# Two attention blocks on one core: where the residual is added, and in which buffers it waits

## The chip, the core and the metric

The kernel runs on one core of a Trainium2 chip. Its engines work in parallel, each on its own queue of instructions: TensorE (PE; PEld is its loading of weights), VectorE (DVE), ScalarE (ACT), GpSimd (POOL) and SyncE (SP), which here issues every DMA. SBUF is the working memory, PSUM the memory that PE writes its products to. GpSimd does not touch PSUM in this kernel. The metric is the device time of one execution in microseconds; the median of several runs counts.

## The reference, cut to what matters

The input x has 8 images of 512 channels and 32 x 32 pixels. Two layers of the same kind follow one another; each is a group normalization, a projection to queries, keys and values, attention with 8 heads of 64 channels over the 1024 pixels, an output projection, and the addition of the layer's input, the residual:

```python
xn = group_norm(x)                       # 8 groups in layer 0, 32 in layer 1
q, k, v = split(qkv_w @ xn + qkv_b)      # each (512, 1024) per image
attn = softmax(q.T @ k / 8)              # per head, 1024 x 1024
out = proj_w @ (attn @ v) + proj_b
return out + x
```

All of it is in float32.

## The kernel before

**Units.** A unit is one layer of one image: units 0 to 7 are layer 0, units 8 to 15 are layer 1. Layer 0 writes its results to `mid` in DRAM, layer 1 to the output. The loop at L903 emits per unit: the values (`v`), the queries (`q`), the keys (`k`), then the output projection of the *previous* unit (`o`), and then the attention of this unit. The first unit has no `o`; the last unit's projection stands alone at the end.

**Products.** Each of v, q, k and o is a 512 x 512 by 512 x 1024 matrix product, done with seven block products in place of eight, in the order 1, 6, 2, 7, 5, 4, 3 (`ORDER`). In q, k and o each of the seven is again done with seven small matmul pairs (`Stream.product`, L411). A product uses one pair of PSUM banks for its main part (`main`, alternating between two pairs, a0 and a1) and another for a part that is the same for half of the result: that part is copied by ACT to the main banks as a seed (L426) and, for the seventh, to a small SBUF tile `late` (L438, three buffers). When the main part is complete, a `finish` step reads it from PSUM on VectorE, and GpSimd then adds `late` to half of the columns (`add_late`, L456 to L458). The tail of a product, with its finish, is emitted inside the product that follows, after that one's first matmul. I write o6 for product 6 of the projection and its finish.

**Sums.** The finishes at L460 to L496 build running sums: p1 (product 1 with bias), u2 = main 6 + p1, u3 = main 7 + bias + u2, and `wide` adds main 5 into u2. These three tiles share two buffers (`accpool`), which attention uses too.

**The output projection** (L537). Its result has four quarters (r, h): r is the half of the channels, h the half of the pixels. For each a tile res[r, h] (128 x 2 x 512) is first loaded with the residual (L546), then the terms are added into it, and it is stored (L558). `take` (L551) adds a product from PSUM on VectorE and `late` on GpSimd; `more` (L555) adds one of the sums, from SBUF to SBUF. Before, `more` runs on VectorE for quarter (0, 0) at o6 and for (0, 1) at o4, and on GpSimd for (1, 1) at o5 and (1, 0) at o4. Below, res10 is the tile of r = 1, h = 0, and so on.

**Buffers.** All four residual tiles come from `ppool`, which has five buffers, and from which come also the rooms xa and xb for combinations of the normalized input (last read by k3), one sum of the values, the rooms oa and ob for combinations of the attention output (last read by o7 and o3), and in attention the exponentials. `tmppool` (one buffer) holds xr, read last by k4, and in attention tmp, written first at step 8; `rbpool` (one buffer) holds the spread reciprocals rb, read last by the division at v5 and written next at step 21 of attention.

**Attention** (L685). 64 steps per unit: eight chunks (a pair of heads and half of the queries) of eight key blocks. A step has scores on PE (L711, eight matmuls), an exponential on ACT (L719) into a `ppool` tile of 128 x 1024, a product with the values on PE (L739, eight matmuls), and a sum of exponentials on VectorE (L758). At the start the order on PE is scores 0, 1, 2, product 0, scores 3, product 1, scores 4 and so on, with products 5 and 6 both ahead of scores 8. An empty PE instruction (`gate`, L108) carries waits that the order alone does not ensure. For step 0 it waits for everything that wrote q and k; in units after the first the keys are long complete then, in unit 0 they are the work just before.

**What sets the order.** It is written out by hand: functions are hung at products with `at(sel, k, ...)` and run after that product's finish, in the order of hanging. Every DMA goes through SP in program order, and an instruction that waits holds those behind it. Residual loads hang at k4, at k3 (two, behind two loads of the next input) and at o7. The statistics of the next input (`stats_of`, L256) hang at o1, o2, o7, o4 and o3. Units 1 to 4 also build a weight image for later units; its raw weights are loaded at L1063 (`load_raw`, four DMAs), between the last product and its tail.

Of the kernel before, what the change touches and what calls it, by code (L numbers as in the profile page):

```python
# [11 lines left out]
F32 = mybir.dt.float32  # L12
# [6 lines left out]
P = 128  # L19
# [13 lines left out]
def fast_path(ctx, tc, x, qkv_wT, proj_wT, vecs, groups, out, flag):  # L33
# [5 lines left out]
    nc = tc.nc  # L39
# [4 lines left out]
    FD = 512  # L44
# [19 lines left out]
    ppool = pool("ppool", 5)  # L64
    accpool = pool("accpool", 2)
    latepool = pool("latepool", 3)
    tmppool = pool("tmppool", 1)
    trpool = pool("trpool", 2)
    rbpool = pool("rbpool", 1)
# [49 lines left out]
    def on(engine, inst, tile_name, *banks):  # L119

        for other, its_engine, its_banks in seen[tile_name]:
            if its_engine != engine and not set(banks) & set(its_banks):
                tc.declare_no_dep(raw(inst), raw(other), reason="another bank of the pair")
        seen[tile_name].append((inst, engine, banks))
        return inst
# [29 lines left out]
    left_slots = [Left(t[:, :, :FD], t[:, :, FD:]) for t in slots]  # L155
# [5 lines left out]
    def load_raw(l, sel, left, ks=tuple(RAW), after=None):  # L161
        w = proj_wT[l] if sel == "o" else qkv_wT[l][:, "qkv".index(sel) * C : ("qkv".index(sel) + 1) * C]
        src = w.rearrange("(c p) o -> p c o", p=P)
        for k in ks:
            c, o = RAW[k]
            n = nc.sync.dma_start(left.outer(k), src[:, c : c + 2, o : o + FD2])
            if after is not None:
                follows(n, after, "x comes first")
                after = None
# [286 lines left out]
    def add_late(t, late):  # L456
        cols = in_two(t[:, 1, :])
        return nc.gpsimd.tensor_add(cols, cols, twice(late))  # L458
# [41 lines left out]
    def make_pairs(stream, w, sel, bias, left, early, hook):  # L500
        l, _ = units[w.u]
        tiles = getattr(w, sel + "p")
        st, p1, u2, u3, wide = sum_steps(l, bias, f"{sel}_{w.u}", early)
        w.last[sel] = []

        def result(r, h, more):
            def finish(main, m, late):
                to = tiles[r][:, :, ts(h, FD)]
                w.last[sel].append(on("DVE", nc.vector.tensor_add(to, main, st[more]), m, 0, 1))
                w.last[sel].append(add_late(to, late))  # L510

            return finish

        def fifth(main, m, late):
            to = tiles[1][:, :, FD:]
            for i in range(2):
                wide(main, m, i)
                w.last[sel].append(
                    on("DVE", nc.vector.tensor_add(to[:, i, :], main[:, i, :], st["u3"][:, i, :]), m, i)
                )  # L520
            w.last[sel].append(add_late(to, late))

        steps = {
            1: p1, 6: u2, 2: result(0, 0, "p1"), 7: u3, 5: fifth, 4: result(1, 0, "u3"),
            3: result(0, 1, "u2"),
        }
        for k in ORDER:
            if k == 1 and early is not None:
                continue

            def finish(main, m, late, k=k):
                steps[k](main, m, late)
                hook(sel, k)

            stream.product(left.quarters(k), w.right.inner[k], k == 3, finish)

    def project(stream, w, left, hook):  # L537
        l, b = units[w.u]
        src, dst = source_of(w.u), mid[b] if l == 0 else out[b]
        st, p1, u2, u3, wide = sum_steps(l, PB, f"o_{w.u}")  # L540
        add = nc.vector.tensor_add
        res = w.res = {}

        def load(r, h):
            t = res[r, h] = ppool.tile([P, 2, FD], F32, tag="p", name=f"res{r}{h}_{w.u}")
            nc.sync.dma_start(t, block_rows(src, r, h))  # L546

        w.load_res = load

        def take(r, h, main, m, late):  # L550
            on("DVE", add(res[r, h], main, res[r, h]), m, 0, 1)  # L551
            add_late(res[r, h], late)

        def more(r, h, name, engine=nc.vector):
            engine.tensor_add(res[r, h], res[r, h], st[name])  # L555

        def store(r, h):
            nc.sync.dma_start(block_rows(dst, r, h), res[r, h])  # L558

        def sixth(*args):  # L560
            u2(*args)
            more(0, 0, "p1")

        def second(*args):
            take(0, 0, *args)
            store(0, 0)

        def fifth(main, m, late):
            t = res[1, 1]
            for i in range(2):  # L570
                wide(main, m, i)
                on("DVE", add(t[:, i, :], main[:, i, :], t[:, i, :]), m, i)
            add_late(t, late)
            more(1, 1, "u3", nc.gpsimd)
            store(1, 1)

        def fourth(*args):
            take(1, 0, *args)
            more(1, 0, "u3", nc.gpsimd)
            store(1, 0)  # L580
            more(0, 1, "u2")

        def third(*args):
            take(0, 1, *args)
            store(0, 1)

        steps = {1: p1, 6: sixth, 2: second, 7: u3, 5: fifth, 4: fourth, 3: third}

        def product(k):
            def finish(main, m, late):  # L590
                steps[k](main, m, late)
                hook("o", k)

            stream.product(left.quarters(k), w.right_o.inner[k], k == 3, finish)

        return product
# [88 lines left out]
    def attention(w, at_step):  # L685
        u = w.u
# [5 lines left out]
        def scores(s):  # L692
            c, t = divmod(s, NT)
            pr, qh = divmod(c, NH)
            if s < 6:
                bank = (*sbank, apair[1])[s % 3]
                before = state["exp"][s - 3 : s - 2] if s >= 3 else []
            elif s == n_steps - 1:
                bank = apair[0]
                before = state["free"][0]  # L700
            else:
                bank = sbank[s % 2]
                before = [state["exp"][s - (3 if s < 8 else 2)]]
            if s < 3:
                before = before + [i for i, _, _ in seen[("s0", "s1", "a1")[s]]]
            if s == 0:
                before += w.last["q"] + w.last["k"]
            gate(*before)
            for j in range(2):
                for e in range(2):  # L710
                    nc.tensor.matmul(  # L711
                        bank[e * H : (e + 1) * H, j, :],
                        w.k[pr][j * H : (j + 1) * H, t * P + e * H : t * P + (e + 1) * H],
                        w.q[pr][j * H : (j + 1) * H, ts(qh, FD)],
                        start=True,
                        stop=True,
                    )
            p = ppool.tile([P, 2, FD], F32, tag="p", name=f"p_{u}_{s}")
            exp = nc.scalar.activation(p, bank, AF.Exp, scale=SCALE)  # L719
            state["exp"].append(exp)  # L720
            state["p"].append(p)
            return p
# [111 lines left out]
        for s in range(n_steps):  # L834
            c, t = divmod(s, NT)
            p = scores(s)
# [39 lines left out]
    first = {sel: mix_left(left) for sel, left in (("v", slot_v), ("q", slot_q), ("k", left_first_k))}  # L876
# [23 lines left out]
    MAKE = {1: (1, "v"), 2: (1, "q"), 3: (1, "k"), 4: (1, "o")}  # L900

    old = None
    for u in range(2 * B):  # L903
        w = Unit()
        w.u, w.right, w.last = u, right, {}
        l, _ = units[u]
# [3 lines left out]
        def at(sel, k, *parts):  # L910
            hooks.setdefault((sel, k), []).extend(parts)
# [124 lines left out]
        ahead = u if last else u + 1  # L1036
        at("k", 5, partial(load_xn, ahead, 0, 2))
        make_pairs(stream, w, "q", QB, lefts["q"], early["q"], hook)
        if u:
            product = project(stream, old, left_slots[1], hook)  # L1040
            at("k", 4, partial(old.load_res, 0, 0))
            at("k", 3, partial(load_xn, ahead, 2), partial(old.load_res, 1, 1), partial(old.load_res, 1, 0))
            at("o", 1, partial(stats_of, 0, 1))
            at("o", 2, partial(stats_of, 2))
            at("o", 7, partial(old.load_res, 0, 1), partial(stats_of, 3, 4))
            at("o", 4, partial(stats_of, 5))
            at("o", 3, partial(stats_of, 6, 7))
        else:
            at("k", 3, partial(load_xn, ahead, 2))
        make_pairs(stream, w, "k", KB, lefts["k"], early["k"], hook)  # L1050
        if u:
            for k in ORDER:
                product(k)
# [4 lines left out]

        right = Right(xn, xt) if not last else None
        making = [] if last else [None] * 8  # L1060
        make = MAKE.get(u)
        if make is not None:
            load_raw(*make, left_slots[0])  # L1063
            making = [part for parts_of in mix_left(left_slots[0])[: 1 if make[1] == "v" else 2] for part in parts_of]

        def at_step(s, state):
# [38 lines left out]
        old = w  # L1105
# [277 lines left out]
```

## Time and profile before

| | |
|---|---|
| median of three runs | 3258.51 us (3257.65 to 3258.57) |
| profiled execution, own time | 3261.41 us |
| its span, first to last instruction | 3259.6 us |
| PE busy | 3208.7 us (98%) |
| VectorE busy | 2862.9 us (88%) |
| ACT busy | 1890.5 us (58%) |
| GpSimd busy | 910.9 us (28%) |

The span is what the trace covers; an execution's own time has a little around it. Times inside the trace count from the span's start. In the rows of groups and of the timeline, `res<-res,u_o` means that a tile named res was written from res and from u_o; the last bracket is idle time of the engine before the instruction, with what ended it. The waits behind a semaphore are inferred from its updates. Busy time of PE is modelled for overlapping matmuls, so a stall can hide in it; the length of a stretch with a known number of steps is the surer measure.

### The profile page before, as it was taken

The numbers are of one execution on the slowest core, as the hardware profiler recorded it, in microseconds if no ns is written. First come the engines' busy times: TensorE is split into PE (matmuls) and PEld (weight loads), VectorE is DVE, ScalarE is ACT, GpSimd is POOL, SyncE is SP. The second block draws the span as 40 slices with busy tenths as digits, with TensorE's granted clock in tenths as the row PEclk, the third lists the DMA queues.
The fourth block names the chain that finished last, engine by engine and source line by source line (L and its number), as shares of the span: only waits on it lengthen the run. The fifth ranks groups of instructions, "written<-read, shape, count | busy, mean of one in ns | idle before, by whom it ended". The sixth has DMA issues, their size and how long they took to land.

```text
span 3259.6 us, 59781 instructions
## 1 busy us (share of the span) xinstructions
PE 3208.7 (98%) x22998; PEld 2087.4 (64%) x22998; DVE 2862.9 (88%) x3362; ACT 1890.5 (58%) x3077; POOL 910.9 (28%) x589
## 2 busy tenths in 40 slices
PE   9999999999999999999999999999999999999999
PEld 7366584765846658476584765857567585675843
DVE  7888989989889898988989889898898988889887
ACT  3655746557465574655656566574655746557454
POOL 5033051330513305133050431504214042240410
PEclk9999999999999999999999999999999999999999
DMA  5333242432424314233142331423323233232311
GB/s 194 107 110 125 78 144 89 145 126 97 141 84 146 123 56 145 77 109 114 52 151 77 106 125 45 156 68 113 115 75 127 74 116 105 85 124 76 127 57 48
DMA packets 151344, 344.83 MB, mean 106 GB/s; under 512 B 27152, under 2 KB 40976, under 8 KB 151056
## 3 DMA queue, kind: packets, MB, share of 16 engines
q1 hardware_dynamic: 151056, 340.94, 32.8%
q8 instruction: 186, 3.05, 0.4%
q14 instruction: 102, 0.84, 0.1%
HBM read 282.29 MB, written 57.02 MB: 104 GB/s over the span
## 4 chain that ended last, share of the span: by engine, by line
PE 89%; POOL 4%; DVE 3%; DMA 2%; ACT 1%; issue 1%; SPq 0%; ACTq 0%; DVEq 0%; POOLq 0%
PE a L739 25%; PE s L711 23%; PE s L421 17%; PE a L421 12%; PE a L398 6%; PE s L398 5%; POOL res L555 2%; POOL res L458 2%; DMA mid<-res 1%; DVE acc L758 1%; DMA out_dram<-res 1%; ACT p L719 1%; PE a L711 0%; PE s L664 0%; PE a L664 0%
## 5 line engine op out<-in xcount | busy, mean ns | idle before, releaser
L719 ACT ACTIVATE p<-s 128x1024 f32<-128x1024 f32 x976 | 997.2, 1024 | 560.6 <-PE s L711 457.0
L739 PE MATMUL a<-p,v 64*64 64x512 f32 x8192 | 1126.6, 590 | 33.8 <-ACT p L719 23.4
L711 PE MATMUL s<-q,k 64*64 64x512 f32 x7808 | 1084.1, 591 | 3.6 <-POOL k L458 3.6
L758 DVE TENSOR_TENSOR acc<-acc,p 128x1024 f32<-128x1024 f32 x768 | 951.6, 1239 | 90.5 <-ACT p L719 45.5
L739 PEld LDWEIGHTS a<-p,v 64*64 64x64 f32 x8192 | 407.5, 131 | 516.7 <-ACT p L719 389.5
L711 PEld LDWEIGHTS s<-q,k 64*64 64x64 f32 x7808 | 430.5, 133 | 390.6 <-issue 390.6
L426 ACT COPY a<-s 128x256 f32<-128x256 f32 x1308 | 465.5, 357 | 278.0 <-PE s L421 197.3
L939 POOL TENSOR_TENSOR k<-xn 128x512 f32<-128x512 f32 x16 | 20.3, 1270 | 1324.1 <-DVE xn L217 1324.1
L438 ACT COPY late<-s 128x256 f32<-128x256 f32 x327 | 121.8, 373 | 179.5 <-PE s L421 179.0
L398 PE MATMUL a<-w,xn 128*128 128x256 f32 x768 | 178.1, 381 | 0.0
L825 ACT ACTIVATE ao<-ao,vec 128x512 f32<-128x512 f32 x128 | 88.4, 715 | 146.9 <-DVE ao L818 146.9
L756 DVE TENSOR_TENSOR acc<-p,p 128x1024 f32<-128x1024 f32 x128 | 162.9, 1272 | 4.2 <-ACT p L719 4.2
L398 PEld LDWEIGHTS a<-w,xn 128*128 128x128 f32 x768 | 144.5, 190 | 31.4 <-issue 12.2
L770 DVE STREAM_TRANSPOSE tr<-acc 128x1024 f32<-128x1024 f32 x128 | 158.0, 1235 | 0.0
L778 DVE TENSOR_REDUCE red<-tr 128x32 f32<-128x1024 f32 x128 | 154.3, 1206 | 0.6
L421 PE MATMUL s<-xn,w 128*128 128x256 f32 x492 | 146.5, 379 | 0.0
L421 PE MATMUL a<-xn,w 128*128 128x256 f32 x492 | 146.4, 379 | 0.0
L421 PE MATMUL s<-k,w 128*128 128x256 f32 x492 | 146.3, 379 | 0.0
L421 PE MATMUL a<-xt,w 128*128 128x256 f32 x462 | 137.5, 379 | 0.0
L288 POOL TENSOR_TENSOR y<-var,half 128x4 f32<-128x4 f32 (+1 forms) x17 | 33.5, 1972 | 366.0 <-DVE var L286 366.0
L765 DVE TENSOR_TENSOR ao<-a,tmp 128x512 f32<-128x512 f32 x128 | 88.1, 688 | 48.9 <-ACT tmp L764 47.8
L421 PE MATMUL s<-xt,w 128*128 128x256 f32 x432 | 128.5, 379 | 0.0
(206 smaller groups left out, 4730.3 us busy)
## 6 DMA issues: line engine op xcount, KB each, us to landing
w<-iq SPq DMA_DIRECT2D x105, 448.0 KB, 3.4
w<-ik SPq DMA_DIRECT2D x105, 448.0 KB, 6.0
w<-io SPq DMA_DIRECT2D x105, 448.0 KB, 3.4
rb<-drec SPq DMA_DIRECT2D x128, 256.0 KB, 3.9
w<-iv SPq DMA_DIRECT2D x105, 256.0 KB, 2.9
xn<-mid SPq DMA_DIRECT2D x36, 512.0 KB, 3.8
xn<-x_dram SPq DMA_DIRECT2D x32, 512.0 KB, 4.2
res<-x_dram SPq DMA_DIRECT2D x32, 512.0 KB, 5.7
```

What stands on the lines that cost most here:

```text
L398: step()
L421: nc.tensor.matmul(dst, a[j], b[j], start=start, stop=j != 1, skip_group_check=True),
L426: n = nc.scalar.copy(dst, one)
L438: on("ACT", nc.scalar.copy(late, seventh), s, 1)
L711: nc.tensor.matmul(bank[e * H : (e + 1) * H, j, :], w.k[pr][j * H : (j + 1) * H, t * P + e * H : t * P + (e + 1) * H], w.q[pr][j * H : (j ...
L719: exp = nc.scalar.activation(p, bank, AF.Exp, scale=SCALE)
L739: nc.tensor.matmul(banks[r][j * H : (j + 1) * H, :], w.v[rows, t, lo : lo + D], p[rows, j, :], start=(t == 0), stop=(t == NT - 1),)
L756: nc.vector.tensor_add(acc, state["first"], p)
L758: nc.vector.tensor_add(acc, acc, p)
L770: nc.vector.transpose(tr, state["acc"].pop(c))
L778: nc.vector.tensor_reduce(red[:, :, qh, :], state["tr"].rearrange("p j (f i) -> p j f i", i=BL), AX.X, ALU.add)
L825: nc.scalar.activation(cols, cols, AF.Identity, bias=vec[:, units[u][0], VB, pr : pr + 1])
```

## The change

Four things change in the program.

1. The residual tiles: res10 now comes from `rbpool` and res01 from `tmppool`; res00 and res11 stay in `ppool`. All four are loaded by k3 (res00 at k4; at k3, behind the two input loads, res10, res11 and res01).
2. The sums: all four `more` additions run on GpSimd, and they come before the takes: p1 into res00 at o1, u2 into res01 at o6, u3 into res10 at o7; u3 into res11 stays at o5. Main 5, which went into u2 and from there into res01, is now added to res01 directly from PSUM at o5, so `wide` is not used there. The number of VectorE instructions at o5 is the same.
3. Two of the eight statistics hang one step earlier (2, 3 at o2; 4, 5 at o7; none at o4), and the raw weights of units 1 to 4 are loaded at o7.
4. The gate of step 0 leaves out the last two writes of the keys (the addition and the late addition of k3, which write pixels 512 to 1023); the gate of step 2 waits for them. Scores 0 to 3 read the first 512 pixels of the keys.

```diff
         def load(r, h):
-            t = res[r, h] = ppool.tile([P, 2, FD], F32, tag="p", name=f"res{r}{h}_{w.u}")
+            room, tag = {(1, 0): (rbpool, "rb"), (0, 1): (tmppool, "tmp")}.get((r, h), (ppool, "p"))
+            t = res[r, h] = room.tile([P, 2, FD], F32, tag=tag, name=f"res{r}{h}_{w.u}")
...
-        def more(r, h, name, engine=nc.vector):
-            engine.tensor_add(res[r, h], res[r, h], st[name])
+        def more(r, h, name):
+            nc.gpsimd.tensor_add(res[r, h], res[r, h], st[name])
...
+        def first(*args):
+            p1(*args)
+            more(0, 0, "p1")
+
         def sixth(*args):
             u2(*args)
-            more(0, 0, "p1")
+            more(0, 1, "u2")
...
+        def seventh(*args):
+            u3(*args)
+            more(1, 0, "u3")
+
         def fifth(main, m, late):
-            t = res[1, 1]
             for i in range(2):
-                wide(main, m, i)
-                on("DVE", add(t[:, i, :], main[:, i, :], t[:, i, :]), m, i)
-            add_late(t, late)
-            more(1, 1, "u3", nc.gpsimd)
+                for t in (res[0, 1], res[1, 1]):
+                    on("DVE", add(t[:, i, :], main[:, i, :], t[:, i, :]), m, i)
+            add_late(res[1, 1], late)
+            more(1, 1, "u3")
             store(1, 1)
 
         def fourth(*args):
             take(1, 0, *args)
-            more(1, 0, "u3", nc.gpsimd)
             store(1, 0)
-            more(0, 1, "u2")
...
-        steps = {1: p1, 6: sixth, 2: second, 7: u3, 5: fifth, 4: fourth, 3: third}
+        steps = {1: first, 6: sixth, 2: second, 7: seventh, 5: fifth, 4: fourth, 3: third}
...
             if s == 0:
-                before += w.last["q"] + w.last["k"]
+                before += w.last["q"] + w.last["k"][:-2]
+            elif s == 2:
+                before += w.last["k"][-2:]
...
-            at("k", 3, partial(load_xn, ahead, 2), partial(old.load_res, 1, 1), partial(old.load_res, 1, 0))
+            at(
+                "k", 3, partial(load_xn, ahead, 2), partial(old.load_res, 1, 0), partial(old.load_res, 1, 1),
+                partial(old.load_res, 0, 1),
+            )
             at("o", 1, partial(stats_of, 0, 1))
-            at("o", 2, partial(stats_of, 2))
-            at("o", 7, partial(old.load_res, 0, 1), partial(stats_of, 3, 4))
-            at("o", 4, partial(stats_of, 5))
+            at("o", 2, partial(stats_of, 2, 3))
+            at("o", 7, partial(stats_of, 4, 5))
             at("o", 3, partial(stats_of, 6, 7))
...
+        make = MAKE.get(u)
+        if make is not None:
+            at("o", 7, partial(load_raw, *make, left_slots[0]))
...
-        make = MAKE.get(u)
         if make is not None:
-            load_raw(*make, left_slots[0])
```

## The prediction

> **What bounds the kernel now.** I read the page first. PE is busy 3208.7 of 3259.6 us, so at most 51 us of visible idle time can be won. The waits by releaser say where it lies (columns: total us, times, longest):
>
> ```profile
> PE a L739 <- ACT p L719: 23.4, 27, 2.7
> PE a L739 <- DVE res L551: 10.4, 14, 0.7
> ...
> PE s L711 <- POOL k L458: 3.6, 1, 3.6
> ACT p L719 <- DMA mid<-res: 54.4, 24, 4.7
> ACT p L719 <- DMA out_dram<-res: 34.1, 20, 4.4
> ```
>
> PE waits for exponentials, and exponentials wait for the stores of residual tiles: the two draw on the same five buffers. Next the timeline of one unit's start of attention (unit 6, scores from 1306.81; start, length, engine, line):
>
> ```profile
> 1305.25 3.18 DVE L555 TENSOR_TENSOR res<-res,u_o 128x1024 f32<-128x1024 f32 x1
> ...
> 1307.29 2.27 POOL L458 TENSOR_TENSOR res<-res,late 128x512 f32<-128x512 f32 x1
> ...
> 1308.95 1.20 DVE L551 TENSOR_TENSOR res<-a,res 128x1024 f32<-128x1024 f32 x1
> 1309.64 2.37 POOL L555 TENSOR_TENSOR res<-res,u_o 128x1024 f32<-128x1024 f32 x1
> ...
> 1310.19 1.02 ACT L719 ACTIVATE p<-a 128x1024 f32<-128x1024 f32 x1 [0.28 <-DMA mid<-res]
> 1310.36 1.09 PE L739 MATMUL a<-p,v 64*64 64x512 f32 x8 [0.74 <-DVE res L551]
> ...
> 1314.83 1.03 ACT L719 ACTIVATE p<-s 128x1024 f32<-128x1024 f32 x1 [3.61 <-DMA mid<-res]
> ...
> 1317.03 1.02 ACT L719 ACTIVATE p<-s 128x1024 f32<-128x1024 f32 x1 [1.17 <-DMA mid<-res]
> ```
>
> Exponentials 2, 3 and 4 wait for the stores of res11, res10, res01 in turn, which GpSimd releases one after another; the first attention product waits for the last take (L551), which stood on VectorE behind the 3.18 us add. Last, the stretches from the first score to the ninth, for units 1 and 6 and the sum over units 1 to 15 (length, then PE busy), and unit 0's start:
>
> ```profile
> 286.94:305.38 18.44, 13.66 (x122) 4.86 (x125) 12.64 (x11) 7.76 (x8) 7.33 (x4) 1.00 0.41 144
> ...
> 1306.81:1321.65 14.84, 13.59 (x122) 4.99 (x124) 12.98 (x11) 7.87 (x8) 7.34 (x4) 1.00 0.28 107
> ...
> sum 237.45, PE 203.69 PEld 74.69 DVE 193.78 ACT 117.70 POOL 109.93; mean PE 13.58 PEld 4.98 DVE 12.92 ACT 7.85 POOL 7.33
> ```
>
> ```profile
> 82.17:85.75 3.58, 0.00 (x1) 0.03 (x1) 3.49 (x3) 0.00 (x0) 2.61 (x2) 0.78 0.01 4
> 85.75:90.89 5.14, 5.14 (x24) 1.67 (x28) 1.14 (x2) 2.05 (x2) 0.00 (x0) 0.50 1.06 408
> 90.89:101.27 10.38, 10.38 (x101) 3.85 (x97) 8.90 (x10) 6.15 (x6) 0.00 (x0) 0.99 0.58 209
> ```
>
> Unit 0 has no residual. From its first attention product to its ninth score (7 products of a step, 5 scores) it needs 10.38 us, 0.865 each, with nothing waiting. Later in attention a step takes 1.72 us and PE does not pause (92.85 busy of 92.85 us in unit 6).
>
> [...] the VectorE add above has two SBUF inputs and took 3.18 us while GpSimd's ran, its like at o6 1.21; L551, with one input in PSUM, took 1.20 to 1.23 always. [...] after 3.58 us idle the granted clock is 0.50 for 5.14 us, and three scores take 5.14 instead of 2.6; the 2.7 us wait of unit 1 leaves 1.00.
>
> **The change, part by part.**
>
> *Added to GpSimd.* Its costs stand in the groups by form (busy us, mean ns of one):
>
> ```profile
> L458 POOL TENSOR_TENSOR res<-res,late 128x512 f32<-128x512 f32 x60 | 106.0, 1767 | 51.8 <-ACT a L426 43.2 <-DVE res L551 8.7
> L555 POOL TENSOR_TENSOR res<-res,u_o 128x1024 f32<-128x1024 f32 x30 | 70.7, 2356 | 2.4
> ...
> L555 DVE TENSOR_TENSOR res<-res,u_o 128x1024 f32<-128x1024 f32 x15 | 47.6, 3174 | 0.0
> ```
>
> Two more wide adds a unit, 2 x 2.36 = 4.7 us, and none on VectorE (1.21 + 3.17 us off it, which bounds nothing but the first product). GpSimd has room where they go: in unit 6 it idled 4.26 us before 1293.59. The order, with 1.27 for an undisturbed late add: p1 is ready at 1291.1; add p1 to 1293.55; late of u2 to 1294.85; add u2 needs res01, now loaded with the others. The second residual there was issued at 1286.81 and took 6.8 us, landing at 1293.6; the loads of that group land 1.2 to 1.3 us apart, so the new third lands at about 1294.9. Add u2 to 1297.3; late of take 0,0 (before: 1296.34 to 1297.6) to 1298.6; late of u3 (VectorE ends u3 at 1299.42) to 1300.7; add u3 to res10 by 1303.1; late of res11, not before 1303.64, to 1304.9; add u3 to res11 to 1307.3, its store issued then: as before. Late of res10 and of res01 are then all that is left: done near 1310 instead of 1314.2.
>
> Who waits: take 1,0 on VectorE now needs the add into res10, 1303.1 against its start at 1304.10; the fifth product's add into res01 (about 1301.6) needs 1297.3; take 0,0 at 1295.04 needs 1293.55. All hold, by 1.0 us at the least. In unit 9 the second residual landed last of all relative to the scores (issued 1888.06, 8.3 us, 1896.4, with scores from 1908.13); shifted to unit 6 the third would land at 1296.4, take 1,0 still 0.3 us ahead. No VectorE instruction with two SBUF inputs is left in the projection after product 1[...]. Late tiles return in time: of three, each is rewritten three products (9 us) on. Cost taken: 0; at worst some tenths a unit.
>
> *Buffers.* res10 takes the room of the reciprocals, free since the division at v5 and next written at step 21; res01 that of xr, read last by product k4 and next written at step 8 of attention, some 13 us after its store is issued. Two residuals stay with the exponentials. Before, buffers were handed out in the order in which they came free: the exponentials met res11, res10, res01 third to fifth. After, a spare one (that of xa or xb), oa, res00, ob and last res11 should be the first five, so exponential 4 waits for res11's store, landing at 1310.1 (1307.4 + 2.7), against 1313 when its scores end. Cost 0.
>
> *The first product* finds take 0,1 ended at about 1308.2 (PE ends the product at 1306.9, add 1.2), needed at 1309.4. The 0.74 us go.
>
> *What units 1 to 15 gain.* Stall free, the stretch is 8 scores + 7 products = 10.38 + 3 x 0.865 = 12.98 us. 237.45 - 15 x 12.98 = **42.8 us** (1.9 in most, up to 5.5 in units that fetch raw weights).
>
> *Moved.* Four raw-weight loads in units 1 to 4 (256 KB, 4.9 us to landing, 3.2 us of SP's issuing together) go from behind the products to o7, at SP behind the store of res00 and ahead of that of res11, 8 us later: hidden, and if not, the slack of exponential 4 covers 3 us. In those units the last store then no longer follows 1 MB. Two statistics (0.68 us each) move: one to o2, after which VectorE idled 1.14 us, one from o4 to o7 into the place of the first: 0. One res load moves from o7 to the k3 group: 0.5 us of SP, counted above.
>
> *Unit 0.* Scores 0 and 1 wait for the keys of product k4 (GpSimd late add 80.71 to 82.75) and go at 82.9; score 2 waits for the last keys, 85.75 as before. Two pauses, 0.7 and 1.1 us, in place of 3.58, so PE should stay at full clock. The first attention product starts at 85.75 + 0.87 = 86.6 instead of 90.89: **4.3 us**; 3.4 if only the two scores move and the slow clock remains.
>
> Sum 47.1. The span gives 3259.6 - 47.1 = 3212.5; the profiled execution's own time, 3261.4, lies 2.9 above the median 3258.5, from which I subtract: 3211.4. I take **3212**.
>
> **Rivals.**
> - *An exponential still waits, or the first product does.* If exponential 0 meets res11's buffer, it ends 4.4 us after the first score, and its product, due at 2.6, loses 1.8 us: 27 us in all, 3238. If take 0,1 stays late by 0.9 us: 13.5, 3225. For it: which buffer is handed out is inferred from one order, and unit 1's differs there (its long wait is at exponential 5). Against: oa and the spare are free long before. 15%, 3222 to 3240.
> - *Unit 0's new order does nothing*, because the scores depend on the whole key tile: 3216. Against: the first matmuls of the kernel read one slice of xn while later slices still load. 7%.
> - *Slower: GpSimd's queue is held by res01's load.* Everything behind add u2 waits, then take 1,0, then ACT's seed of the next product in that bank pair. From the working above, take 1,0 is late once the load lands after 1296.7; about 1.2 us more are absorbed, since a pair's next product is one product (3.02 us) away; each further microsecond costs one per unit. The gain of 2.85 a unit is spent at about 1301, 14 us after issue; no residual load took over 8.3. At 17 us: 45 us lost, 3303. 6%.
> - *Nothing, or under 10 us*, because VectorE's sums, 1.24 of 1.72 us a step, become the bound when PE comes early. Against: unit 0's stretch ran unstalled with VectorE 8.90 busy of 10.38. 4%.
>
> **Numbers.** The forecast's own case, 68%, spans 3205 (units 1 to 4 gain later too, where step 13 takes 0.5 us longer) to 3219. 8 in 10 with unit 0's rival and the nearer half of the first: 3205 to 3230. Differences under 0.2%, 6.5 us, can hardly be told from no change. Faster 0.92, same 0.02, slower 0.06.
>
> **What would show it.** Right: no waits of exponentials for residual stores; the sum of the fifteen stretches near 195; four L555 adds a unit on GpSimd at 2.36 and no VectorE ones; the second before 1295.5 in unit 6's terms; clock 1.0 in unit 0's start. Wrong: exponentials with waits of 1 us or more on a store, take 1,0 waiting for GpSimd, PE pausing inside the projection, or the late adds of GpSimd still running 5 us into attention.

## The result, and the profile after

The changed kernel takes 3211.77 us (median of four runs, 3211.28 to 3213.12) against 3258.54 us (3257.65 to 3260.96) for the kernel before: the ratio is 0.9856, 95% interval 0.9839 to 0.9873, or 46.8 us less. The forecast was 3212, inside 3205 to 3230. The span went from 3259.6 to 3211.3 us, 48.3 less.

The waits of PE by releaser, changed kernel (columns as before: total us, times, longest). L719 is now the line of the scores, L747 that of the product with the values, L727 the exponential, L552 the take, L556 the wide additions:

```profile
PE s L332 <- DMA xn<-x_dram: 4.5, 1, 4.5
PE s L398 <- DVE u_v L646: 1.2, 3, 0.8
...
PE a L719 <- POOL k L458: 0.9, 1, 0.9
PE s L719 <- POOL k L458: 0.7, 1, 0.7
```

The product with the values is gone from this view: neither an exponential nor a take holds it anywhere. What is left of unit 0's wait for its keys is 0.7 and 0.9 us. The waits of ACT list no exponential that waits for the landing of a residual's store, where this was 88.5 us.

The timeline of unit 6's start of attention, changed kernel (scores from 1280.96; PE's own rows before that left out):

```profile
1278.29 1.22 DVE L552 TENSOR_TENSOR res<-a,res 128x1024 f32<-128x1024 f32 x1 [0.57 <-ACT a L426]
...
1279.21 2.35 POOL L556 TENSOR_TENSOR res<-res,u_o 128x1024 f32<-128x1024 f32 x1
...
1281.12 1.22 DVE L552 TENSOR_TENSOR res<-a,res 128x1024 f32<-128x1024 f32 x1 [1.60 <-PE a L421]
1281.52 2.52 POOL L458 TENSOR_TENSOR res<-res,late 128x512 f32<-128x512 f32 x2
...
1283.59 1.04 PE L747 MATMUL a<-p,v 64*64 64x512 f32 x8
```

The last take begins as soon as PE has the product, 0.16 us after the first score (it was 2.14), and ends at 1282.34. The first product with the values starts 2.63 us after the first score (it was 3.55). GpSimd's last addition ends at 1284.04, 3.1 us after the first score, where it was 7.4.

The stretches from the first score to the ninth, changed kernel, for units 1 and 6 and the sum of units 1 to 15, and then unit 0's start (length, PE busy, and so on as before):

```profile
283.85:296.78 12.93, 12.93 (x123) 4.67 (x125) 10.19 (x10) 7.98 (x8) 3.09 (x3) 1.00 0.32 124
...
1280.96:1293.89 12.93, 12.93 (x122) 4.67 (x125) 10.18 (x10) 7.99 (x8) 3.08 (x3) 1.00 0.32 123
...
sum 193.95, PE 193.95 PEld 70.06 DVE 151.79 ACT 119.82 POOL 46.61; mean PE 12.93 PEld 4.67 DVE 10.12 ACT 7.99 POOL 3.11
```

```profile
84.13:86.99 2.86, 1.95 (x16) 0.60 (x17) 2.86 (x3) 1.71 (x2) 2.05 (x1) 1.00 0.01 6
86.99:87.87 0.88, 0.88 (x8) 0.39 (x12) 0.88 (x2) 0.23 (x1) 0.00 (x0) 1.00 1.04 407
```

All fifteen stretches are 12.93 us, with PE busy throughout: 237.45 - 193.95 = 43.5 us. In unit 0 PE ended the keys at 82.17 before and at 83.40 now (those 1.2 us are already lost 12 us into the span, long before anything that was changed); from there to the first product with the values it was 8.72 and is 4.47 us, and the clock stays at 1.00. 43.5 and 4.3 make 47.8 of the 48.3 us of the span. The remaining half microsecond is a sum of small differences of both signs elsewhere: unit 0's keys 1.2 us later; the products ahead of unit 4's attention 1.2 us less, and unit 3's attention 1.2 us less, where before PE had run at half its clock for 3.4 us after a pause of 2.37 us.

### The profile page after: what moved, and what is told of

The parts are those of the page before. It is cut to its first block, busy times and chain, and to the rows that moved or that the text cites. A ratio compares the mean times of both kernels' runs of the same rounds, so it can differ in the third digit from the quotient of the medians.

```text
span 3211.3 us, 59784 instructions
## 1 busy us (share of the span) xinstructions
PE 3196.2 (100%) x22998; PEld 2031.7 (63%) x22998; DVE 2776.9 (86%) x3332; ACT 1892.7 (59%) x3077; POOL 931.0 (29%) x619
## 4 chain that ended last, share of the span: by engine, by line
PE 94%; DVE 4%; issue 1%; DMA 1%; ACT 0%; SPq 0%; POOL 0%; DVEq 0%; ACTq 0%
PE a L747 25%; PE s L719 24%; PE s L421 18%; PE a L421 13%; PE a L398 6%; PE s L398 5%; DVE acc L766 2%; PE a L719 1%; PE s L670 0%; DMA lt<-red 0%; PE a L670 0%; DVE tr L778 0%; DVE red L786 0%; DVE acc L764 0%; DVE ao L773 0%
## 5 line engine op out<-in xcount | busy, mean ns | idle before, releaser
L727 ACT ACTIVATE p<-s 128x1024 f32<-128x1024 f32 x976 | 998.2, 1024 | 523.1 <-PE s L719 489.7
L747 PE MATMUL a<-p,v 64*64 64x512 f32 x8192 | 1105.6, 589 | 0.0
L719 PE MATMUL s<-q,k 64*64 64x512 f32 x7808 | 1063.8, 590 | 0.7 <-POOL k L458 0.7
L766 DVE TENSOR_TENSOR acc<-acc,p 128x1024 f32<-128x1024 f32 x768 | 938.5, 1222 | 76.6 <-ACT p L727 33.6
L747 PEld LDWEIGHTS a<-p,v 64*64 64x64 f32 x8192 | 389.3, 131 | 489.7 <-ACT p L727 345.9
L719 PEld LDWEIGHTS s<-q,k 64*64 64x64 f32 x7808 | 394.5, 133 | 421.4 <-issue 421.4
L764 DVE TENSOR_TENSOR acc<-p,p 128x1024 f32<-128x1024 f32 x128 | 152.7, 1193 | 9.4 <-ACT p L727 9.4
L288 POOL TENSOR_TENSOR y<-var,half 128x4 f32<-128x4 f32 (+1 forms) x17 | 26.0, 1530 | 382.7 <-DVE var L286 378.3
```

The source lines that it names most:

```text
L719: nc.tensor.matmul(bank[e * H : (e + 1) * H, j, :], w.k[pr][j * H : (j + 1) * H, t * P + e * H : t * P + (e + 1) * H], w.q[pr][j * H : (j ...
L747: nc.tensor.matmul(banks[r][j * H : (j + 1) * H, :], w.v[rows, t, lo : lo + D], p[rows, j, :], start=(t == 0), stop=(t == NT - 1),)
L764: nc.vector.tensor_add(acc, state["first"], p)
L766: nc.vector.tensor_add(acc, acc, p)
```

## The experiments

**The gates alone.** The kernel before with this edit:

```diff
-                before += w.last["q"] + w.last["k"]
+                before += w.last["q"] + w.last["k"][:-2]
+            elif s == 2:
+                before += w.last["k"][-2:]
```

> The kernel before with the two changed gates alone. The forecast's step: two short pauses in place of 3.58 us, clock at 1.0 in unit 0's start, 4.3 us less than before (3254.2). Rival, the scores depend on the whole key tile: no change (3258.5) and the 3.58 us wait still there. Units 1 to 15 keep their stretch sum of 237 us in both.

Measured: 3257.97 us beside 3260.61 for the kernel before in the same runs, ratio 0.9991 (0.9982 to 0.9999). By the ratio that is 2.9 us less, with an interval from 0.3 to 5.9. The times alone can hardly size it, the trace can. PE in the kernel with the gates alone (L713 the scores, L741 the product with the values):

```profile
84.88 1.95 PE L713 MATMUL s<-q,k 64*64 64x512 f32 x16 [0.73 <-POOL k L458]
87.74 1.09 PE L713 MATMUL a<-q,k 64*64 64x512 f32 x8 [0.92 <-POOL k L458]
88.62 1.07 PE L741 MATMUL a<-p,v 64*64 64x512 f32 x8
```

The two pauses are those of the forecast, in place of 3.58 us, and the scores run at full rate (16 matmuls in 1.95 us, where before 24 took 5.14): from the end of the keys (84.15) to the first product it is 4.47 us instead of 8.72. The span is 4.6 us shorter. The gate does what it says: the scores don't depend on the whole key tile.

**The rooms alone.** The kernel before with the `load` hunk of the change and nothing else.

> The kernel before with the two residual tiles in their new rooms alone; sums, loads and gates as before. The forecast's theory: no exponential waits for a store any more, the first product still waits 0.74 us (0.9 with what follows) for the last take, stretches 13.85 us each, sum 208: 3229. Rival A, the rooms carry all of it: stretches 13.0, 3216. Rival B, the shorter GpSimd chain carries it and the rooms only make the early load possible: over 3250.

Measured: 3229.1 us, ratio 0.9901 (0.9886 to 0.9916). The waits of PE in this kernel (L740 the product with the values, L552 the take, L712 the scores):

```profile
PE a L740 <- DVE res L552: 9.9, 13, 0.9
...
PE s L712 <- POOL k L458: 3.6, 1, 3.6
```

The stretches are 13.86 to 13.90 us in most units, as worked out. With other buffers for two tiles the exponentials' waits for stores go, from 88.5 us to none in the waits of ACT, although the additions keep their slow old order; what stays is the first product, behind a take that VectorE reaches late, and unit 0's wait for its keys.

**One addition put back on VectorE, late.** The changed kernel with this edit:

```diff
         def sixth(*args):
             u2(*args)
-            more(0, 1, "u2")
...
             take(1, 0, *args)
             store(1, 0)
+            nc.vector.tensor_add(res[0, 1], res[0, 1], st["u2"])
```

> The changed kernel with one addition put back: u2 goes into res01 on VectorE after take 1,0. Theory: that addition waits for GpSimd's wide one (until about 0.5 us after the first score), take 0,1 ends 2.9 us after the first score and the first product, due at 2.6, waits some 0.45 us a unit: 7 us more, 3219. Rival, VectorE's place does not matter since the first product is bound by its exponential: 3212, no wait of the product for the take.

Measured: 3220.39 us, ratio 0.9874 (0.9859 to 0.9889), 8.6 us above the changed kernel. GpSimd, VectorE and PE at unit 6 of this kernel (scores from 1284.40; L587 is the addition put back, L552 the take):

```profile
1282.59 2.35 POOL L556 TENSOR_TENSOR res<-res,u_o 128x1024 f32<-128x1024 f32 x1
1282.88 3.13 DVE L587 TENSOR_TENSOR res<-res,u_o 128x1024 f32<-128x1024 f32 x1
...
1286.15 1.23 DVE L552 TENSOR_TENSOR res<-a,res 128x1024 f32<-128x1024 f32 x1
...
1287.58 1.09 PE L747 MATMUL a<-p,v 64*64 64x512 f32 x8 [0.38 <-ACT p L727]
```

The VectorE add runs beside GpSimd's and takes 3.13 us instead of 1.2; the take ends at 1287.38 and the product follows at 1287.58, 3.18 us after the first score. The bracket names an exponential, but the one that this product needs began at 1285.56 and lasts 1.02, so it had been done for a microsecond: the take is what ended the wait. The stretches are 13.5 us, 0.57 above 12.93; times 15 that is the 8.6.

**Does res01 need its own room?** The changed kernel with `(0, 1)` left out of the table in `load`.

> The changed kernel with res01 back among the exponentials' buffers. Theory B (the order of the sums is enough): its store lands 5.9 us after the first score, its buffer is the fifth to be met, by exponential 4 at 6.1 us: 3212 to 3215. Theory A (the rooms are what counts): exponentials wait 1.5 us or more a unit, 3235 or more.

Measured: 3212.12 us, ratio 0.985 (0.9835 to 0.9865): as the changed kernel. Its exponentials still wait 10.3 us for stores in all, 8.3 of them in layer 1, but PE waits 0.2 us for them. So with the earlier additions one room, res10's, is enough, where with the old order both rooms together ended these waits: the order covers the gain of the second room, and the gains of the parts don't add. This run is not the order alone; the next one is.

**What the rooms are needed for.** The new order with no extra room, all four tiles among the exponentials' buffers:

```diff
-            room, tag = {(1, 0): (rbpool, "rb"), (0, 1): (tmppool, "tmp")}.get((r, h), (ppool, "p"))
+            room, tag = {}.get((r, h), (ppool, "p"))
```

> The changed kernel with all four residual tiles among the exponentials' five buffers. Theory: the exponentials still meet stores that have landed, but only three buffers are free when the residuals are loaded; the fourth, res01, waits for oa, which PE reads until product o7, lands some 8 us later and holds GpSimd's queue as in the run with three loads: 5 us a unit, 3275 to 3300. Rival, the allocation finds room another way or GpSimd's queue has slack: under 3225.

Measured: 3277.99 us, ratio 1.0065 (1.0049 to 1.0082). SP's own waits (L547 the loads of the residual) and GpSimd at unit 6 (two views of this kernel):

```profile
SPq L547 <- PE a L421: 153.6, 15, 10.3
```

```profile
1286.81 1.27 POOL L458 TENSOR_TENSOR u_o<-u_o,late 128x512 f32<-128x512 f32 x1
1295.84 2.34 POOL L556 TENSOR_TENSOR res<-res,u_o 128x1024 f32<-128x1024 f32 x1 [7.76 <-DMA res<-x_dram]
```

The load of res01 waits some 10 us a unit for PE to finish with a buffer; GpSimd's queue stands for 7.8 us with all that is behind it. Two of the forecast's steps meet here: a tile outside the five buffers is what lets res01 be loaded early, and an early load is what the early addition lives on. Together with the run before it shows that one tile outside is enough. The time came as expected, but not all of the theory: the exponentials do wait for stores again, 43.7 us in all (88.5 in the kernel before), and PE 9.8 us for them. Whether the missing room or the late queue of GpSimd brings these waits back, no run here separates.

**The load made late by itself.** The changed kernel with res01 loaded three times:

```diff
-            nc.sync.dma_start(t, block_rows(src, r, h))
+            for _ in range(3 if (r, h) == (0, 1) else 1):
+                nc.sync.dma_start(t, block_rows(src, r, h))
```

> The changed kernel with res01 loaded three times over, each load waiting for the one before, so that the tile is complete some 7 to 8 us later (about 1302 to 1303 in unit 6's terms of the prediction) and nothing else changes. The slower rival's rule (each microsecond after 1298 costs one per unit): 4 to 5 us a unit, 3272 to 3287, with PE pausing inside the projection. Rival, GpSimd's queue and three late tiles absorb it: under 3225.

Measured: 3292.22 us, ratio 1.0097 (1.0082 to 1.0113), 80.5 us above the changed kernel or 5.4 a unit. VectorE in unit 6 of this kernel (L581 the fifth product's adds, L553 the take, L557 the wide additions), then ACT and PE:

```profile
1302.81 2.48 DVE L581 TENSOR_TENSOR res<-a,res 128x512 f32<-128x512 f32 x4 [4.30 <-POOL res L557]
1307.68 1.22 DVE L553 TENSOR_TENSOR res<-a,res 128x1024 f32<-128x1024 f32 x1 [2.39 <-POOL res L557]
```

```profile
1304.04 0.37 ACT L438 COPY late<-s 128x256 f32<-128x256 f32 x1 [4.32 <-POOL res L458]
1304.74 1.22 PE L421 MATMUL a<-ot,w 128*128 128x256 f32 x2 [3.26 <-ACT a L426]
```

GpSimd began the addition at 1300.44, 16.2 us after the first residual of its group was issued; in the changed kernel it is 8.9 us. VectorE waits for it twice, but PE is held by another path: ACT's copy to a `late` tile needs one of the three buffers, and GpSimd gives it back only with the late addition that stands behind the wide one in its queue (it ends at 1304.00). ACT's seed and PE come after that copy. All fifteen projections have this wait of ACT, 67.4 us together, and PE pauses in each, 2.3 to 4.9 us.

The pauses make 51.4 of the 76.7 us by which the span is longer. Most of the rest is PE's clock, 0.991 on average over this execution where it is 1.000 in the changed kernel. The pause and the time from there to the first score, in unit 6 and in unit 11:

```profile
1301.48:1304.74 3.26, 0.00 (x1) 0.00 (x1) 1.93 (x4) 0.70 (x3) 3.26 (x3) 0.84 0.00 0
1304.74:1310.80 6.06, 6.06 (x14) 4.41 (x15) 1.78 (x2) 1.94 (x6) 5.90 (x4) 0.52 0.22 87
2319.13:2322.41 3.28, 0.00 (x1) 0.00 (x1) 1.93 (x4) 0.70 (x3) 3.28 (x3) 1.00 0.00 0
2322.41:2325.91 3.50, 3.48 (x14) 2.49 (x15) 1.10 (x2) 1.94 (x6) 3.42 (x3) 1.00 0.39 150
```

The same pause is followed by 6.06 us at a clock of 0.52 in one unit and by 3.50 us at 1.00 in the other. Thirteen of the fifteen pauses are followed by half the clock.

The forecast's rule gives 4.4 us for this landing. Its slope holds: in this run and the one before, in all thirty projections, PE's pause is the start of the addition into res01 less 9.48 us, counted from the projection's first sum (L466), to 0.02 us. But PE begins to pause only with an addition that starts at 1299.3 in unit 6's terms of the prediction, that is with a landing at 1299.1, which is 1.2 us later than the rule had it; and the rule has no term for the clock after the pause.

**The raw weights put back.** The changed kernel with the four loads of units 1 to 4 behind the products, as before.

> The changed kernel with the raw weights of units 1 to 4 loaded where they were before. The forecast: the move is worth nothing once no exponential shares a buffer with the last store, 3211 to 3213. Rival, part of what units 1 to 4 gained comes from moving these loads: 2 to 5 us in each of the four, 3220 to 3232.

Measured: 3212.58 us (3211.76 to 3213.27), ratio 0.9852 (0.9836 to 0.9867), the stretches of units 1 to 4 12.93 us as the others. The move is worth nothing that shows.

**All four additions on VectorE.** The changed kernel with one word exchanged:

```diff
-            nc.gpsimd.tensor_add(res[r, h], res[r, h], st[name])
+            nc.vector.tensor_add(res[r, h], res[r, h], st[name])
```

> The changed kernel with all four additions in their new places but on VectorE. Theory, the place counts more than the engine: VectorE is late by up to 3 us at take 1,0 and some tenths at take 0,1, 3212 to 3219. Rival, VectorE is full in the projection and PE waits for its takes: over 3225.

Measured: 3255.78 us, ratio 0.9983 (0.9977 to 0.999). The expectation missed, and the time lies where its rival had it: nearly the whole gain is gone, though the same additions run in the same places, on an engine that takes 1.23 us for one instead of 2.36. VectorE in unit 6 of this kernel, then the largest wait of PE:

```profile
1284.29 1.23 DVE L556 TENSOR_TENSOR res<-res,u_o 128x1024 f32<-128x1024 f32 x1 [1.38 <-POOL u_o L458]
...
1290.60 1.23 DVE L556 TENSOR_TENSOR res<-res,u_o 128x1024 f32<-128x1024 f32 x1 [1.45 <-POOL u_o L458]
...
1296.83 1.23 DVE L556 TENSOR_TENSOR res<-res,u_o 128x1024 f32<-128x1024 f32 x1 [1.43 <-POOL res L458]
```

```profile
PE s L421 <- ACT a L426: 29.7, 42, 1.8
```

Three of the four additions need a tile to which GpSimd must first add a `late`; VectorE waits for that, in order, with the takes behind it: 4.26 us in this unit. With 15.56 us of work these waits fill the 19.85 us from the projection's first sum to the first score (17.02 us in the changed kernel), and ACT's seeds, with PE behind them, come late. My expectation had counted only VectorE's busy time. On GpSimd the same addition stands behind the late one in the same queue: in the changed kernel the idle time before all 45 of them is 11.0 us, in fifteen units together. To tell this wait from an engine that is simply full, a second kernel does the same work on VectorE with each of the three one finish later:

```diff
             u2(*args)
-            more(0, 1, "u2")
...
             take(0, 0, *args)
             store(0, 0)
+            more(0, 1, "u2")
...
             u3(*args)
-            more(1, 0, "u3")
...
             add_late(res[1, 1], late)
-            more(1, 1, "u3")
-            store(1, 1)
+            more(1, 0, "u3")
...
             take(1, 0, *args)
             store(1, 0)
+            more(1, 1, "u3")
+            store(1, 1)
```

> The kernel with all four additions on VectorE as in the run before, but each of the three that follow a late addition by GpSimd hung one finish later (u2 into res01 behind take 0,0; u3 into res10 behind the fifth product's adds; u3 into res11 behind take 1,0), when that late addition should be done. VectorE's work is the same as in the run before. If the 44 us lost there came from VectorE waiting in order for GpSimd's late additions (1.4 us three times a unit), most of them come back: 3212 to 3235. If VectorE is simply too full in the projection: 3245 or more, with little of its idle time ended by GpSimd.

Measured: 3219.99 us, ratio 0.9883 (0.9866 to 0.9899): 35.8 of the 44.0 us come back, with the same work on VectorE, so most of the loss was the wait. The same wait of PE is now

```profile
PE s L421 <- ACT a L426: 4.5, 14, 0.3
```

The other 8.2 us go with VectorE's load: fourteen projections take 17.61 us from the first sum to the first score, 0.59 more than in the changed kernel, and the fifteenth, in which no statistics are left to compute, takes 17.02. That load is also what makes the wait costly. The fifteenth projection of the kernel with the waits has them too, 1.46, 1.44 and 1.43 us in the same three places, and takes 17.23 us where most others take 19.84.

**The gates moved further.** The changed kernel with

```diff
-                before += w.last["q"] + w.last["k"][:-2]
-            elif s == 2:
-                before += w.last["k"][-2:]
+                before += w.last["q"] + w.last["k"][:2]
+            elif s == 4:
+                before += w.last["k"][2:]
```

> The changed kernel with the gates moved further: step 0 waits for the keys of product k2 alone, step 4 for all the others (steps 0 to 3 read only the first half of the first two pairs' keys). Theory: both pauses of unit 0's start, 0.7 and 0.9 us, go, 1.6 us less, 3210.2, which the trace can show better than the times. Rival: the first exponentials or the a1 banks take their place, no change.

Measured: 3210.2 us (3208.5 to 3210.28), ratio to the kernel before 0.9843 (0.9829 to 0.9856). No run is above any of the changed kernel's, and in the trace unit 0's scores follow the keys with no pause, its stretch 12.93 us instead of 14.04. This is the fastest version, by about 1.6 us, 0.05%.

## Why the prediction was right

- *The total.* The sum of 47.1 us stands beside 48.3 in the spans and 46.8 in the medians. That 3212 and 3211.77 agree to a quarter of a microsecond is luck beyond this: the profiled execution lay 2.9 us above the median before and 1.4 us after.
- *The buffers.* Right: no exponential waits for a store. But the prediction did not ask whether both means were needed. Both rooms with the old order leave PE 0.4 us of waiting for exponentials, and the new order with one room leaves 0.2 us; the new order with no room leaves 9.8 us and, by its late load, makes the kernel slower than before. The rival in which a wait for a buffer stays did not come.
- *The first product.* Right, in the term's size too: it was forecast at 0.9 us with what follows it; the rooms alone leave 13.87 - 12.93 = 0.94 us a unit. The last take ends 1.38 us after the first score, forecast 1.4.
- *The sum over units 1 to 15.* 42.8 forecast, 43.5 measured. The difference is the stall-free stretch, 12.93 us instead of the 12.98 taken from unit 0, times 15.
- *GpSimd's timetable.* Right to some tenths. The groups by form of the changed kernel:

```profile
L556 POOL TENSOR_TENSOR res<-res,u_o 128x1024 f32<-128x1024 f32 x45 | 106.2, 2360 | 11.0 <-DMA res<-mid 4.0 <-DMA res<-x_dram 2.8 <-PE s L421 1.6
L458 POOL TENSOR_TENSOR res<-res,late 128x512 f32<-128x512 f32 x60 | 76.1, 1279 | 7.7 <-ACT a L426 7.7
```

Two more wide additions a unit at 2.36 us, as the row of before said. The late additions fell from 1767 to 1279 ns on average, what the prediction called undisturbed. In the trace of before, of the sixty, the fifteen that ran beside VectorE's wide addition (L555, two SBUF inputs) took 2.26 to 2.28 us, the fifteen beside the sums of exponentials (L756, L758) 2.25 to 2.28, and the other thirty, at most beside takes (L551) and statistics (L256), 1.27. In the changed kernel, where no addition of two SBUF tiles is left on VectorE in the projection after product 1, all sixty take 1.27 to 1.29. The third load landed 11.7 us before the first score in unit 6, forecast 11.9; the row puts 6.8 us of GpSimd's waiting, in all fifteen units together, down to residual loads.
- *The slower rival.* It did not happen, and it was real: with res01 7.3 us later the kernel is slower than before. Its working was off in three places. The path: it led from the load over take 1,0 to the seed in the same bank pair, and the prediction had the late tiles return in time; what holds PE is a late tile that does not. The threshold: 1299.1 for the landing and not 1297.9, 1.2 us too early, so the changed kernel has more slack than forecast. The price: one microsecond for each microsecond of pause, with nothing for the clock after it. The last two errors work against each other, so it is partly luck that the forecast's 4.4 us a unit lies near the measured 5.4.
- *The engine.* The prediction put VectorE's relief at nothing beyond the first product, and that is what one addition put back late shows. But it did not see why the early additions belong on GpSimd: with them on VectorE in the same places the change is worth 0.17% rather than 1.4%.
- *Unit 0.* 4.3 us forecast; 4.25 in the trace of both kernels with the new gates.
- *Moved loads and statistics.* Put at nothing, and the raw weights measured at nothing. The moved statistics were not tested alone.

## What to carry to other kernels

When work is moved between engines, count the waits it will have in the queue, not its duration alone: an addition that takes 1.23 us on one engine and 2.36 on another was worth 44 us less on the faster one, because there it had to wait in order for a neighbour that on the slower engine runs just ahead of it (4.26 us in unit 6), and that engine had no slack for the wait. If buffers of a ring are held by something that leaves late, either give that thing other rooms or make it leave earlier, and try the parts one by one, since their gains may overlap: here the second room added 0.35 us to the new order. If early work rests on an early load, ask which free buffer that load needs, because a load without one holds every queue that waits for it: GpSimd's stood for 7.8 us in unit 6 with all tiles shared. And when a pause of PE is priced, look at the clock after it as well as at its length: two pauses of 3.3 us were followed by 0.52 and by 1.00 here.

## What the hardware showed that I had not expected

The price of one and the same pause of PE differs between executions. In the kernel before and in the one with the rooms alone PE stands for 3.58 us ahead of unit 0's scores. Before, the granted clock was already at 0.78 on average within the pause and at 0.50 for the 5.14 us after it; with the rooms alone it is (the pause, then the first two scores):

```profile
82.44:86.02 3.58, 0.00 (x1) 0.03 (x1) 3.49 (x3) 0.00 (x0) 2.62 (x2) 1.00 0.01 4
86.02:88.74 2.72, 2.72 (x16) 1.04 (x20) 0.80 (x1) 1.02 (x1) 0.00 (x0) 0.61 1.05 409
```

Here the clock fell only after the pause, and the stretch to the ninth score was 14.59 us instead of 15.52: 0.9 us between two executions of one unit. Pauses of 0.73 and 0.91 us in the changed kernel, with 2 us of work between them, left the clock at 1.00.

Nor does the longer pause always cost more. In the kernel before, unit 1's pause of 2.69 us leaves the clock at 1.00 for the 3.42 us after it, while unit 3's, 2.37 us long, is followed, 1.29 us after its end, by 3.41 us at 0.50. With all four tiles shared, here are two stretches around a pause of 2.02 us (685.56 to 687.58), then one with a pause of 2.04 us (889.10 to 891.14) and the one after it:

```profile
683.64:687.05 3.41, 1.92 (x9) 1.34 (x8) 1.40 (x3) 0.33 (x2) 3.41 (x3) 1.00 0.01 2
687.05:690.46 3.41, 2.87 (x13) 2.21 (x13) 1.09 (x2) 2.11 (x7) 3.33 (x3) 1.00 0.76 231
888.44:891.85 3.41, 1.37 (x7) 0.89 (x6) 2.48 (x4) 1.20 (x4) 3.33 (x4) 1.00 0.16 61
891.85:895.26 3.41, 3.41 (x9) 2.72 (x9) 1.16 (x1) 0.83 (x3) 3.41 (x2) 0.50 0.94 272
```

Around the first pause the clock stays at 1.00; after the second, 0.02 us longer, 3.41 us run at 0.50. So the length of a pause does not settle it here, and the 2.7 us of unit 1, which the prediction saw leave the clock at 1.00, are no safe limit: 2.04 us were enough, while the 3.28 us of unit 11 above did not lower it. What decides between two such pauses, no run here separates.
